# Part products of three image rows: another order for the second image, three products of half width for the third and last

## The chip, the cores and the metric

The kernel runs on one core of a Trainium2 chip. A core has five engines that run beside each other, each with its own queue of instructions in a fixed order: TensorE (PE, matrix products, with weight loads shown as PEld), VectorE (DVE), ScalarE (ACT), GpSimd (POOL) and SyncE (SP, which here only issues transfers). An engine waits at the head of its queue until what it needs is there; everything behind it waits too. The metric is the device time of one execution in microseconds (us), the median of several runs; smaller is better.

## What is computed

The input x has four images of 256 channels and 64 x 64 pixels, in 32-bit floats. Two layers follow each other.

1. Local attention. A 7 x 7 convolution with dilation 2 (128 outputs, then a 1 x 1 convolution to 49) gives 49 logits for each pixel; a softmax over the 49 gives weights; the output at a pixel is the sum of the 49 dilated neighbours of x, each by its weight:

```
k = conv(x, w1, dilation 2, padding 6) + b1        # 4 x 128 x 64 x 64
k = conv(k, w2, 1 x 1) + b2                        # 4 x 49 x 64 x 64
attn = softmax(k, over the 49)
y[b, c, h, w] = sum over (u, v) of x_padded[b, c, h + 2u, w + 2v] * attn[b, (u, v), h, w]
```

2. Whitening. The 256 channels of y are taken in four groups of 64. Each group's covariance over all pixels of all images is formed, its inverse square root is found by five Newton steps, and the group's channels are multiplied by it.

## The kernel before

Both convolutions are merged into one with 49 outputs of 7 x 7 taps over 256 channels. Because the dilation is 2, rows and columns of equal parity form four independent convolutions of 32 x 32 pixels. Each is done by a fast convolution in two dimensions (Toom-Cook): rows and columns are evaluated at seven points 0, 1, -1, 2, -2, 1/2 and infinity (`EVAL`, `INF = 6`), products are taken for each pair of a row point and a column point, and the output is interpolated, first along columns (`col_interp`), then along rows (`row_interp`).

**Row points.** For the row points 1, -1, 2, -2, 1/2 (and 0 for the later images) a row of products is made in three banks (`conv_bank`, matmuls at line 604, two halves of the partitions for the two row parities): DVE makes the column points (`xh`), PE multiplies, ACT copies the result out of PSUM into `pv` (lines 615 and 620), and DVE interpolates it into `zz`. The row points at infinity, and 0 in the first two images, need no evaluation of rows. There the 7-tap convolution along the columns is taken directly from the pixels: `direct` does it with seven products of whole rows (matmuls at line 779). `direct_part` (matmuls at line 862) does it with three products of half width, in two column classes: with even and odd column pairs x0 and x1 and even and odd taps w0 and w1, part 1 is w1 on x0, part 2 is w0 on x1, and part 3 is the sum of both tap classes on the sum of both pixel classes. `direct_sums` makes the sums on DVE, and `direct_ends` puts the three products together (ACT copies part 1, DVE adds part 2 twice and subtracts from part 3). In the kernel before, the second image uses the three products for its row points infinity and 0; the third and fourth use `direct`, called from `direct_inf`.

**Order of the work.** Images overlap. While image b is convolved, image b - 1 goes through softmax (`soft`), through the moves of its weights into a band shape (ACT copies into `zt` at line 1253, stores to `sd` in DRAM issued by POOL at line 1272, loads of `band` and `bandz` issued by SP at lines 1322 and 1334), and through the weighted sum on PE (line 1442, with blocks of pixels that PE has transposed at line 1378), whose results are turned (line 1514) and multiplied into the covariance (line 1533). A list of steps with costs per image (line 1703 and on) places the pieces of image b - 1 between the convolution steps of image b; `steps.insert` puts the direct rows and the softmax at its start. Within that frame a scheduler orders the instructions of each engine by priority. On DVE part of the order is written out: `add`, `sub` and `madd` (lines 345 to 352) go through `in_turn`, which makes each of them stand behind the last one that was issued while `strict` was on. `in_order` turns `strict` on around an image's last interpolations (`col_interp`, then `row_interp(b, 1)`).

**Memory that the change touches.** `spare` is the third part of `pv`; its first 686 elements hold the weights of the row at infinity of the next image (`kept[INF]`, loaded by SP at line 899), and the part behind them is a temporary of `col_interp`. `lgx` holds the weights of the second image's row 0 (`gr0`) while they are needed, and the logits of an image afterwards. `acc` are two banks of PSUM that the weighted sums use later; `conv_psum()` gives the two convolution banks in turn. `tap`, `gbr` and `gb5` lie in a pool (`gpool`) that is released at the end of the front part, and whose memory then holds `zt`, `band` and the softmax terms.

Of the kernel before, what the change touches and what calls it, by code (L numbers as in the profile page):

```python
# [9 lines left out]
F32 = mybir.dt.float32  # L10
# [13 lines left out]
INF = 6  # L24
# [8 lines left out]
def kernel(  # L33
# [310 lines left out]
    def add(o, a, b):  # L344
        return in_turn(TT(o, a, b, ALU.add))  # L345
# [409 lines left out]
    def direct(b, br, s, ps, w, xr=None):  # L755


        a = 3 if br == INF else 0
        order = [(v, cc) for v in sorted(range(KS), key=lambda v: abs(v - R)) for cc in range(NCC)]
        for j, (v, cc) in enumerate(order):  # L760
            d = 2 * (v - R)
            w0, w1_ = max(0, -d), min(W, W - d)
            for h in range(2):
                if xr is not None:
                    parts = [(w0, w1_, xr[:, :, h, cc, w0 + d : w1_ + d])]
                elif b == 0:
                    xs = slots[h].rearrange("p c (q a) w -> p a q c w", a=4)[:, a]
                    parts = [(w0, w1_, xs[:, :, cc, w0 + d : w1_ + d])]
                else:
                    xs = halves(slots[2 * b + h])[:, cc].rearrange("p h (q a) w -> p a h q w", a=4)  # L770
                    parts = []
                    for g in range(2):
                        i0, i1 = max(w0 + d, g * SW), min(w1_ + d, (g + 1) * SW)
                        parts.append(
                            (i0 - d, i1 - d, xs[:, a, g, :, i0 - g * SW : i1 - g * SW])
                        )
                for k, (o0, o1, rhs) in enumerate(parts):
                    pe(
                        nc.tensor.matmul(  # L779
                            ps[h * HB : h * HB + KT, :, o0:o1],  # L780
                            w[v][:, cc],
                            rhs,
                            start=(j == 0 and k == 0),
                            stop=(j == len(order) - 1),
                            skip_group_check=True,
                        )
                    )
        z = zz[:K2, br]
        if s == 0:
            with tc.high_priority():  # L790
                nc.scalar.copy(z[:, :Q8], ps[:K2])
        else:

            def second():
                nc.scalar.copy(z[:, Q8], ps[:K2, Q8 - 1])
                add(z[:, 1:Q8], z[:, 1:Q8], ps[:K2, : Q8 - 1])

            if br == 0 and b == 0:

                seconds.append(second)  # L800
            else:
                second()

    M16, NX = W // 4, Q8 * 2 * NCC * W // 2

    def direct_sums(b, br, w, room):

        a = 3 if br == INF else 0
        xs = []
        for h in range(2):  # L810
            x = slots[2 * b + h].rearrange("p c r w -> p (c r w)").rearrange(
                "p (e a w) -> p a e w", a=4, w=SW
            )
            x = x[:, a].rearrange("p e (m i two) -> p i e m two", i=2, two=2)
            o = room[:, h * NX // 2 : (h + 1) * NX // 2]
            add(o.rearrange("p (e m two) -> p e m two", m=SW // 4, two=2), x[:, 0], x[:, 1])
            xs.append(
                o.rearrange("p (c g q w) -> p c g q w", c=NCC, g=2, q=Q8).rearrange(
                    "p c g q (m two) -> p c g q m two", two=2
                )  # L820
            )
        ws = []
        for s, t in enumerate(w):
            nw = (KS // 2) * NCC * KT
            o = room[:, NX + s * nw : NX + (s + 1) * nw]
# [50 lines left out]
    def direct_view(ps, n, m):  # L876
        return ps.rearrange("p q w -> p (q w)")[:, : n * m * 2].rearrange(
            "p (q m two) -> p q m two", q=n, two=2
        )

    def direct_ends(br, n, p1, p2, p3=None):

        z = zz[:K2, br, :n].rearrange("p q (m i two) -> p i q m two", i=2, two=2)
        if p3 is None:
            nc.scalar.copy(z[:, 0], p1[:K2])
            add(z[:, 1], z[:, 0], p2[:K2, :, 1:])
            add(z[:, 0], z[:, 0], p2[:K2, :, :M16])
        else:
            sub(z[:, 1], p3[:K2], z[:, 1])
# [3 lines left out]
    def conv_psum():  # L893
        ncv[0] += 1
        return cv_buf[(ncv[0] - 1) % 2].rearrange("p (q w) -> p q w", w=W)

    def direct_inf(b):

        nc.sync.dma_start(spare[:, :NTAP], kept[INF])
        t = spare[:, :NTAP].rearrange("p (v a k) -> p v a k", v=KS, a=NCC)  # L900
        direct(b, INF, 0, conv_psum(), [t[:, v] for v in range(KS)])

    start_of = {}

    def direct_start(sr):

        n = Q8 + 1
        w = [[gr0[:, v, :, s] for s in range(2)] for v in range(KS)]
        if sr == 0:
            room = store[4].rearrange("p c r w -> p (c r w)")[:, SH * W :]  # L910
            xs, ws = direct_sums(1, 0, [[t[s] for t in w] for s in range(2)], room)
            start_of["xs"] = xs
            start_of["ws"] = [[t[j] for t in ws] for j in range(KS // 2 + 1)]
# [10 lines left out]
    acc = [ps_y.tile([P, Q8, W], F32, tag="y", name=f"acc{sr}") for sr in range(2)]  # L924
    for a in acc:
        nc.vector.memset(a, 0.0)
# [779 lines left out]
    for b in range(1, B):  # L1706

        steps = []
        for k, (bk, br) in enumerate(rows):
            if bk == b:  # L1710
                for i, cost in enumerate((6, 5, 2)):
                    steps.append((cost, lambda k=k, i=i: conv_step(k, i)))
        if b == 1:
            for sr in range(2):
                steps.insert(sr, (12, lambda sr=sr: direct_start(sr)))
            steps.insert(0, (0, lambda: soft(0, 0)))
            steps.insert(3, (0, lambda: soft(0, 1)))
        else:
            steps.insert(0, (12, lambda b=b: direct_inf(b)))
        j, at, whole = 0, 0, sum(c for c, _ in steps)  # L1720
        for cost, f in steps:
            half_next[0] = (at + cost) * NPC >= (j + 1) * whole and (b, j) in half_gaps
            f()
            while rest_of:
                rest_of.pop()()
            at += cost
            if at * NPC >= (j + 1) * whole:
                gap(b, j)
                j += 1
                while after_gap:  # L1730
                    after_gap.pop()()
# [302 lines left out]
```

## Time and profile before

| what | value |
| --- | --- |
| median of 3 runs | 668.89 us (668.85 to 669.1) |
| profiled execution | 668.98 us, span of its instructions 667.2 us |
| mean granted clock of PE | 0.991 |
| second image's row at infinity: parts 2 and 1 (112 matmuls), part 3 (64) | 6.36 us, 3.49 us |
| second image's row 0: parts 2 and 1 (224 matmuls) | 12.42 us |
| third and fourth image's row at infinity: `direct` (112 matmuls each) | 273.02 to 284.61 and 409.00 to 420.58 us |
| first weighted sum on PE | 186.57 us |

One matrix product of 32-bit floats is two matmul instructions in the trace. A row of the profile gives its start, its length, the engine, the line of the kernel, the operation with what it writes and reads, the shape, the count of merged instructions, and in brackets how long the engine had stood idle and what ended that. Lines 345, 348 and 352 are the helpers `add`, `sub` and `madd`, so these rows are told apart by the tile that they write.

### The profile page before, as it was taken

Reading aid. Unit: us, or ns where it says so; the run is one execution under the profiler, and the core shown is the slowest. Engines: PE = TensorE matmul, PEld = TensorE weight load, DVE = VectorE, ACT = ScalarE, POOL = GpSimd, SP = SyncE. Lnnn points to the kernel's source line nnn. Section 1 sums busy time; section 2 is a strip of 40 time slices with the busy share of each in tenths; the row PEclk is TensorE's granted clock in tenths of the full one; section 3 lists DMA queues with packets and bytes.
Section 4 is the critical chain, followed back from the end, with each engine's and each line's share of the span. In section 5 each row is a group of like instructions: output and inputs, shape, how many; then the busy total and the mean of one; then the engine's idle time right before and its main releaser. Section 6 shows DMA issues by size and latency. Waiting matters only on the chain.

```text
span 667.2 us, 19415 instructions
## 1 busy us (share of the span) xinstructions
PE 638.7 (96%) x7992; PEld 530.1 (79%) x7992; DVE 571.2 (86%) x1258; ACT 331.8 (50%) x861; POOL 115.3 (17%) x173
## 2 busy tenths in 40 slices
PE   6999999999999999999999999999999999999991
PEld 1439673358999998889999998999999999997440
DVE  3699999999899889999999799989999988634781
ACT  1434331013565566467754554473855667535681
POOL 0000551663213002001022020002220203500000
PEclk9999999999999999999999999999999999999996
DMA  8961799995599988324588673026364325739698
GB/s 316 247 177 67 128 232 382 218 195 83 133 205 223 228 257 304 103 57 108 149 278 278 232 246 107 1 69 195 103 197 112 70 65 129 182 96 380 263 412 335
DMA packets 109840, 126.11 MB, mean 189 GB/s; under 512 B 69127, under 2 KB 92216, under 8 KB 107576
## 3 DMA queue, kind: packets, MB, share of 16 engines
q1 hardware_dynamic: 92952, 69.35, 35.5%
q0 software_dynamic: 10752, 37.26, 21.7%
q10 hardware_dynamic: 6048, 18.27, 8.8%
q8 instruction: 63, 1.03, 0.7%
q14 instruction: 25, 0.20, 0.1%
HBM read 78.78 MB, written 52.36 MB: 197 GB/s over the span
## 4 chain that ended last, share of the span: by engine, by line
PE 62%; DVE 17%; issue 7%; POOL 4%; SPq 4%; DMA 3%; ACT 2%; DVEq 0%; ACTq 0%; POOLq 0%
PE cv L604 25%; PE y L1442 13%; PE sig L1533 5%; PE tp L1514 4%; PE tp L1378 4%; SPq L225 4%; POOL ahead L147 2%; POOL slot L147 2%; PE tp L1844 2%; PE cv L862 2%; DVE zz L352 2%; DVE rb L345 2%; PE cv L779 2%; DVE xh L352 2%; DVE pv L352 1%
## 5 line engine op out<-in xcount | busy, mean ns | idle before, releaser
L604 PE MATMUL cv<-xh,wr 128*49 128x128 f32 x4160 | 232.3, 273 | 0.1
L604 PEld LDWEIGHTS cv<-xh,wr 128*49 128x49 f32 x4160 | 226.2, 124 | 2.9 <-issue 1.0
L1272 POOL DMA_DIRECT2D sd<-zt x120 | 63.3, 534 | 292.2 <-ACT zt L1253 222.2
L1442 PE MATMUL y<-band,xb 128*128 128x209 f32 x448 | 93.7, 341 | 0.6 <-ACT xb L1409 0.6
L1442 PEld LDWEIGHTS y<-band,xb 128*128 128x128 f32 x448 | 75.7, 191 | 1.5 <-ACT xb L1409 0.8
L615 ACT COPY pv<-cv 113x486 f32<-113x486 f32 (+2 forms) x60 | 25.9, 431 | 82.4 <-PE cv L604 82.2
L352 DVE SCALAR_TENSOR_TENSOR pv<-pv 113x162 f32<-113x162 f32 x176 | 52.5, 320 | 1.5 <-ACT pv L615 1.0
L1524 ACT COPY yt<-tp 128x512 f32<-128x512 f32 x60 | 35.0, 591 | 24.3 <-PE tp L1514 23.5
L1253 ACT COPY zt<-d 32x112 f32<-32x112 f32 (+2 forms) x132 | 38.6, 293 | 11.0 <-DVE d L1123 5.1
L1514 PE MATMUL tp<-ident,slot 128*128 128x128 f32 x240 | 41.3, 295 | 0.2 <-ACT slot L1464 0.2
L1378 PE MATMUL tp<-ident,slot 128*128 128x128 f32 x256 | 40.5, 282 | 0.0
L1175 ACT ACTIVATE d<-tp,mx 128x49 f32<-128x49 f32 x96 | 27.4, 321 | 24.2 <-DVE mx L1172 17.6
L1533 PE MATMUL sig<-yt 128*64 128x65 f32 x1024 | 38.0, 225 | 0.9 <-ACT yt L1524 0.9
L1514 PEld LDWEIGHTS tp<-ident,slot 128*128 128x128 f32 x240 | 34.9, 205 | 5.0 <-issue 3.7
L1378 PEld LDWEIGHTS tp<-ident,slot 128*128 128x128 f32 x256 | 38.2, 204 | 0.2 <-issue 0.2
L1533 PEld LDWEIGHTS sig<-yt 128*64 128x64 f32 x1024 | 32.9, 137 | 6.7 <-issue 1.9
L1409 ACT COPY xb<-tp 128x512 f32<-128x512 f32 x52 | 30.6, 588 | 13.7 <-PE tp L1378 10.5
L352 DVE SCALAR_TENSOR_TENSOR xh<-ct 128x512 f32<-128x512 f32 x40 | 26.6, 691 | 5.7 <-PE cv L604 5.4
L147 POOL DMA_DIRECT2D slot<-in_x_dram x12 | 20.4, 1701 | 53.4 <-DVE xh L352 38.6
L348 DVE TENSOR_TENSOR pv<-pv 113x162 f32<-113x162 f32 (+1 forms) x77 | 27.5, 364 | 0.3
L352 DVE SCALAR_TENSOR_TENSOR xh<-xh,rb 128x512 f32<-128x512 f32 x40 | 27.4, 684 | 0.1
L345 DVE TENSOR_TENSOR ct<-rb 128x1024 f32<-128x1024 f32 (+1 forms) x26 | 26.5, 1020 | 0.3
(288 smaller groups left out, 1141.9 us busy)
## 6 DMA issues: line engine op xcount, KB each, us to landing
band<-sd SPq DMA_DIRECT2D x64, 242.0 KB, 3.6
sd<-zt POOLq DMA_DIRECT2D x120, 77.0 KB, 4.2
wr<-gd ACTq DMA_DIRECT2D x14, 588.0 KB, 4.8
wr<-gd ACTq DMA_DIRECT2D x14, 490.0 KB, 4.1
slot<-in_x_dram POOLq DMA_DIRECT2D x12, 512.0 KB, 10.5
ahead<-in_x_dram POOLq DMA_DIRECT2D x12, 512.0 KB, 7.8
spill<-slot POOLq DMA_DIRECT2D x3, 2048.0 KB, 9.4
slot<-ahead POOLq DMA_DIRECT2D x3, 2048.0 KB, 10.7
```

What stands on the lines that cost most here:

```text
L147: yield queue.dma_start(o[:, cc, h], src[:, :, pr, h * SW : (h + 1) * SW])
L345: return in_turn(TT(o, a, b, ALU.add))
L352: return in_turn(STT(o, a, f, b, ALU.mult, ALU.add))
L604: nc.tensor.matmul(o, wv[:, sc, sr, cc], xv[bc][:, h * NCC + cc], start=(j == 0), stop=(j == len(terms) - 1), skip_group_check=True,)
L1253: ins = nc.scalar.copy(o, i)
L1272: dma = queue.dma_start(bass.AP(tensor=D.tensor, offset=D.offset + h * HS + g * RS, ap=[[LS, TC], [CR * RS, NCH], [1, KS * WS]],), zt[p0 : ...
L1378: nc.tensor.transpose(t[:, h * C + cc * P : h * C + (cc + 1) * P], tile_of(xt, cc, t8, h, pc), turned_by(n),)
L1409: (nc.vector.tensor_copy if n > 4 * B - 3 else nc.scalar.copy)(xb.rearrange("p a c -> p (a c)"), t[:, : 2 * C])
L1442: nc.tensor.matmul(y_ps[n, half, cc][:, q0 : q0 + nq, c0:c1], xb[:, cc * P : (cc + 1) * P], rhs, start=(k == 0), stop=(k == len(PIECES[hal ...
L1514: nc.tensor.transpose(t[:, h * C + cc * P : h * C + (cc + 1) * P], tile_of(yt, cc, t8, h, pc), turned_by(n),)
L1524: return nc.scalar.copy(yb.rearrange("p h a g c -> p (h a g) c")[:, :, :GW], t[:, : 2 * C].rearrange("p (e c) -> p e c", c=GW),)
L1533: nc.tensor.matmul(sig[g * GW : (g + 1) * GW, cc], yb[:, g, :GW], yb[:, g], start=(count[0] == 0), stop=end, skip_group_check=True,)
```

## The change

It has three parts. First, the second image: the parts 2 and 1 of its row at infinity are taken earlier, straight after the first image's last direct product, and the sums for its part 3 are made after the first image's row interpolation, into `spare` and the last third of `lgx`; part 3 itself moves behind the parts 2 and 1 of row 0, into `direct_start(1)` (`third_inf`). Second, the step of the first softmax, `soft(0, 0)`, moves from before `direct_start(0)` to behind it. Third, `direct_inf` of the third and the last image makes the three products of half width in place of the seven whole ones: parts 1 and 2, then part 3 in the bank of part 1, with the sums in the free part of `pv` and behind the weights in `spare`, and a memset on POOL that restores the zeros there. Besides, the tap sums are made by one addition (`direct_taps`) where there were three or six.

```diff
-    def direct_sums(b, br, w, room):
+    def direct_sums(b, br, w, room, sums):
...
-        ws = []
-        for s, t in enumerate(w):
-            nw = (KS // 2) * NCC * KT
-            o = room[:, NX + s * nw : NX + (s + 1) * nw]
-            o = o.rearrange("p (v a k) -> p v a k", v=KS // 2, a=NCC)
-            for j in range(KS // 2):
-                add(o[:, j], t[2 * j + 1], t[2 * j])
-            ws.append([o[:, j] for j in range(KS // 2)] + [t[KS - 1]])
-        return xs, ws
+        return xs, direct_taps(w, sums)
+
+    def direct_taps(w, sums):
+
+        n = w.shape[2]
+        o = sums[:, : KS // 2 * n].rearrange("p (v n) -> p v n", n=n)
+        pair = w[:, : KS - 1].rearrange("p (v two) n -> p two v n", two=2)
+        add(o, pair[:, 1], pair[:, 0])
+        return [o[:, j] for j in range(KS // 2)] + [w[:, KS - 1]]
...
         nc.sync.dma_start(spare[:, :NTAP], kept[INF])
         t = spare[:, :NTAP].rearrange("p (v a k) -> p v a k", v=KS, a=NCC)
+        if b in (2, 3):
+            free = pv[:, 1 - (len(slot) - NV) % 2]
+            with tc.high_priority():
+                xs, ws = direct_sums(
+                    b, INF, t.rearrange("p v a k -> p v (a k)"),
+                    free.rearrange("p n q b -> p (n q b)"), spare[:, NTAP:],
+                )
+            one = lambda t: [t.rearrange("p (a k) -> p a k", a=NCC)]
+            p2 = direct_view(conv_psum(), Q8, M16 + 1)
+            bank = conv_psum()
+            p1 = direct_view(bank, Q8, M16)
+            w = [[t[:, v]] for v in range(KS)]
+            direct_part(b, INF, 1, p1, w)
+            direct_part(b, INF, 2, p2, w)
+            with tc.high_priority():
+                direct_ends(INF, Q8, p1, p2)
+            p3 = direct_view(bank, Q8, M16)
+            direct_part(b, INF, 3, p3, [one(t) for t in ws], xs)
+            with tc.high_priority():
+                direct_ends(INF, Q8, None, None, p3)
+            nc.gpsimd.memset(
...
+            )
+            return
         direct(b, INF, 0, conv_psum(), [t[:, v] for v in range(KS)])
...
         else:
-            p3 = direct_view(acc[0], n, M16)
+            third_inf()
+            p3 = direct_view(acc[1], n, M16)
             direct_part(1, 0, 3, p3, start_of["ws"], start_of["xs"])
             direct_ends(0, n, None, None, p3)
 
+    def third_inf():
+
+        p3 = direct_view(acc[0], Q8, M16)
+        direct_part(1, INF, 3, p3, start_of["ws_inf"], start_of["xs_inf"])
+        direct_ends(INF, Q8, None, None, p3)
...
     prepare(NR0, 0)
-    w = [tap[:, UPOS[3], v] for v in range(KS)]
-    xs, ws = direct_sums(1, INF, [w], gbr.rearrange("p v a s k -> p (v a s k)"))
     direct0(5, 1)
+    g = tap[:, UPOS[3]].rearrange("p v a k -> p v (a k)")
+    one = lambda t: [t.rearrange("p (a k) -> p a k", a=NCC)]
+    p2 = direct_view(acc[0], Q8, M16 + 1)
+    direct_part(1, INF, 2, p2, [one(g[:, v]) for v in range(KS)])
+    p1 = direct_view(acc[1], Q8, M16)
+    direct_part(1, INF, 1, p1, [one(g[:, v]) for v in range(KS)])
     row_interp(0, 1)
-
-    w = [[t] for t in w]
-    p2 = direct_view(acc[0], Q8, M16 + 1)
-    direct_part(1, INF, 2, p2, w)
-    p1 = direct_view(acc[1], Q8, M16)
-    direct_part(1, INF, 1, p1, w)
-    p3 = direct_view(conv_psum(), Q8, M16)
-    direct_part(1, INF, 3, p3, [[t] for t in ws[0]], xs)
+    direct_ends(INF, Q8, p1, p2)
+    room = lgx[:, 2 * KS * NCC * KT :]
+    start_of["xs_inf"], ws = direct_sums(1, INF, g, spare, room)
+    start_of["ws_inf"] = [one(t) for t in ws]
     prepare(NR0, 1)
     prepare(NR0, 2)
     strict[0] = False
-    direct_ends(INF, Q8, p1, p2)
-    direct_ends(INF, Q8, None, None, p3)
+    last_tap = room[:, KS // 2 * NCC * KT :][:, : NCC * KT]
+    nc.scalar.copy(last_tap, g[:, KS - 1])
+    start_of["ws_inf"][-1] = one(last_tap)
     gpool.release()
...
         if b == 1:
             for sr in range(2):
                 steps.insert(sr, (12, lambda sr=sr: direct_start(sr)))
-            steps.insert(0, (0, lambda: soft(0, 0)))
+            steps.insert(1, (0, lambda: soft(0, 0)))
             steps.insert(3, (0, lambda: soft(0, 1)))
```

More of the change, by code (lines that the diff above doesn't have):

```diff
@@ L900, in direct_inf @@
         t = spare[:, :NTAP].rearrange("p (v a k) -> p v a k", v=KS, a=NCC)
+        if b in (2, 3):
[19 more added lines that the diff above has]
+            nc.gpsimd.memset(
+                free[:, ORDER.index(INF)].rearrange("p q b -> p (q b)").rearrange(
+                    "p (q c) -> p q c", q=Q9
+                )[:, :, 2 * Q8 :],
+                0.0,
+            )
+            return
         direct(b, INF, 0, conv_psum(), [t[:, v] for v in range(KS)])
+    acc = [ps_y.tile([P, Q8, W], F32, tag="y", name=f"acc{sr}") for sr in range(2)]
+    for a in acc:
+        nc.vector.memset(a, 0.0)
     start_of = {}
@@ L907, in direct_start @@
         n = Q8 + 1
-        w = [[gr0[:, v, :, s] for s in range(2)] for v in range(KS)]
         if sr == 0:
+            by_share = lambda t: [
+                t.rearrange("p (a s k) -> p a s k", a=NCC, s=2)[:, :, k] for k in range(2)
+            ]
+            g = lgx[:, : KS * 2 * NCC * KT].rearrange("p (v n) -> p v n", v=KS)
             room = store[4].rearrange("p c r w -> p (c r w)")[:, SH * W :]
-            xs, ws = direct_sums(1, 0, [[t[s] for t in w] for s in range(2)], room)
+            xs, ws = direct_sums(1, 0, g, room, room[:, NX:])
             start_of["xs"] = xs
-            start_of["ws"] = [[t[j] for t in ws] for j in range(KS // 2 + 1)]
+            start_of["ws"] = [by_share(t) for t in ws]
+            w = [by_share(g[:, v]) for v in range(KS)]
             p2 = direct_view(conv_psum(), n, M16 + 1)
@@ L919, in direct_start @@
         else:
-            p3 = direct_view(acc[0], n, M16)
+            third_inf()
+            p3 = direct_view(acc[1], n, M16)
             direct_part(1, 0, 3, p3, start_of["ws"], start_of["xs"])
             direct_ends(0, n, None, None, p3)
-    acc = [ps_y.tile([P, Q8, W], F32, tag="y", name=f"acc{sr}") for sr in range(2)]
-    for a in acc:
-        nc.vector.memset(a, 0.0)
+    def third_inf():
+        p3 = direct_view(acc[0], Q8, M16)
+        direct_part(1, INF, 3, p3, start_of["ws_inf"], start_of["xs_inf"])
+        direct_ends(INF, Q8, None, None, p3)
     rows = [(0, br) for br in (1, 2, 3)]
```

## The prediction

> **What bounds the kernel now.** I read the page's busy shares first, then busy time by stage, then the order of time of PE and DVE around the three changed places, and last what ended each engine's waits. Busy shares of the 667.2 us span, then three stages (after the range and its length: busy us of PE, PEld, DVE, ACT and POOL with counts, then the granted clock):
>
> ```profile
> PE 638.7 (96%) x7992; PEld 530.1 (79%) x7992; DVE 571.2 (86%) x1258; ACT 331.8 (50%) x861; POOL 115.3 (17%) x173
> ...
> 176.80:273.00 96.20, 94.75 (x1409) 91.71 (x1409) 86.94 (x202) 59.09 (x158) 13.77 (x26) 1.00 0.93 235
> 273.00:285.00 12.00, 12.00 (x123) 9.12 (x118) 12.00 (x35) 2.54 (x6) 0.00 (x0) 1.00 0.21 73
> 285.00:409.00 124.00, 123.18 (x1808) 119.42 (x1808) 117.25 (x242) 77.45 (x222) 17.03 (x32) 1.00 0.61 194
> ```
>
> From 142 us to about 545 us PE hardly waits, so PE work taken away there is time, and so is every new wait put into its queue. But DVE is nearly as full: in the stage 273 to 285, where the third image's row at infinity runs, it has no gap at all. So a sum that the change gives to DVE counts as soon as PE needs it at once. PE in order of time (start, length, what; in brackets its wait):
>
> ```profile
> 142.50 6.36 PE L862 MATMUL acc<-slot,tap 128*49 128x128 f32 x112
> 149.80 2.72 PE L862 MATMUL cv<-gbr 128*49 128x128 f32 x48 [0.94 <-DVE gbr L345]
> 154.94 1.21 PE L1135 MATMUL tp<-ident,slot 113*128 113x113 f32 x8 [1.65 <-ACT slot L746]
> ...
> 186.57 0.98 PE L1442 MATMUL y<-band,xb 128*128 128x209 f32 x4
> ...
> 273.02 11.66 PE L779 MATMUL cv<-slot,pv 128*49 128x256 f32 x112
> ```
>
> DVE at the ends of the images' row interpolation (the lgx rows), and the two places where it last waited for PE before:
>
> ```profile
> 247.52 0.64 DVE L352 SCALAR_TENSOR_TENSOR wr<-ct 128x196 f32<-128x196 f32 x2 [2.71 <-PE cv L604]
> 284.51 0.69 DVE L352 SCALAR_TENSOR_TENSOR lgx<-zz 113x512 f32<-113x512 f32 x1
> ...
> 382.44 0.69 DVE L352 SCALAR_TENSOR_TENSOR xh<-ct 128x512 f32<-128x512 f32 x1 [4.33 <-PE cv L604]
> 418.42 0.69 DVE L352 SCALAR_TENSOR_TENSOR lgx<-zz 113x512 f32<-113x512 f32 x1
> ```
>
> These waits tie DVE's clock to PE's: if PE is late, DVE is late too, and the lag between them at the lgx rows stays as it is.
>
> **Part 1: the third image's row at infinity.** Removed: 112 matmuls of about 256 columns, 273.02 to 284.61, 11.6 us. Added: 176 of half width. The second image's same row gives the price: its parts 2 and 1 (112 matmuls) took 6.36 us, its part 3 (64) 3.49 us, both together 9.9 us. So PE's own work falls by 1.7 us.
>
> But part 3 needs two sums of pixels and one of weights from DVE. They pass through the helper that holds DVE's written order, and in the built order they stand right after the last step of the row interpolation, the lgx row at 284.51. That step gives way after 0.61 us (distance to the next row), at 285.1. Then two sums of 512 (1.21 us, the distance that the two gbr sums took at 148.02), one addition of 256 (0.33, from 160.59 to 160.92) and the weight sum of 294 elements (0.45, between the rows of 162 with 0.32 and 324 with 0.49): 287.1. PE has finished parts 1 and 2 at 273.0 + 6.4 = 279.4 and has nothing else to do: the third product stands next in its queue, and all later matmuls behind it. It waits 7.7 us, runs 3.5 us, and is done at 290.6 instead of 284.6: 6.0 us late. A wait of 0.57 us for ACT at 288.29 goes, since ACT has time meanwhile. **Step: +5.5 us.**
>
> DVE pays 2.6 us more than before here (the sums above, 0.33 for the second addition, 0.4 for the subtraction of part 3), yet PE is 5.5 us late, and at 382.44 DVE had 4.3 us to spare. So this costs nothing more. ACT copies 256 elements instead of 512: less work. POOL gets a memset of 18 elements after part 3; it issued nothing from 255 to 312 us, nor from 391 to 450 behind the last image's. SP's load of the next image's weights moves from 284.7 to about 290.7 and the store behind it on SP moves along; the weights are wanted at 409, so this is hidden.
>
> **Part 2: the last image, same steps.** Parts 1 and 2: 409.0 + 6.4 = 415.4. The lgx row at 418.42 gives way at 419.0; sums until 421.0; part 3 until 424.5, instead of 420.6. The wait is 5.6 us. **Step: +4.0 us.** DVE is tied to PE at 382 to 386, so the lag is that of before.
>
> **Part 3: the second image.** PE's queue now runs: infinity parts 2 and 1 (to 148.9), first row's parts 2 and 1 (12.4, to 161.3), eight transposes for the first softmax (1.2), infinity part 3 (3.5), first row's part 3 (6.7), four and eight transposes (1.7): convolution starts at 174.6 and not at 176.83. The waits of 0.94 and 1.65 us go; 2.2 us are gained, and the 88 products before the first weighted sum (9.74 us) end at 184.4.
>
> The first softmax, however, now stands behind 12.4 us of products on PE, and DVE's maximum of it behind steps that used to come later. DVE from 148.02: interpolation tail 4.3, two additions 0.7, infinity sums 1.6, column steps of ct and xh 4.5, first row's sums 1.2 + 0.7 (one addition of 588 where six of 98 were), three rb and ct steps 4.5: the maximum at 165.4 (before: 155.91). Maximum 1.0, sixteen exponentials 4.6, scaling 1.6, shuffles 3.1: ready at 176.0 (before 166.73), 9.3 us late. Behind it hangs this chain (ACT copies, POOL stores, SP loads of the band):
>
> ```profile
> 166.84 3.33 ACT L1253 COPY zt<-d 128x56 f32<-128x56 f32 x11 [5.11 <-DVE d L1123]
> ...
> 169.62 4.21 POOL L1272 DMA_DIRECT2D sd<-zt  x8 [12.66 <-issue]
> ...
> 176.94 0.91 SPq L1322 DMA_DIRECT2D band<-sd  x2
> ```
>
> All 9.3 us later: band issued at 186.2, landed 3.7 us after (median of the band loads in 165 to 192), at 189.9. Before, it landed at about 180.6, and PE first used it at 186.57: 6 us of cover. Now PE is there at 184.4 and waits 5.5 us. **Step: 189.9 - 186.57 = +3.3 us**; ends: -2.2 us if the band is in time, +5 us if the band takes 5.4 us to land, between that median and the longest of all, 8.1. The weight load for the third image moves on SP from 126.5 to about 166, is wanted at 273, and costs nothing.
>
> **Part 4: PE's clock after a wait.** No wait of PE in the middle of this trace reaches 2 us, and the granted clock is 1.00 throughout. What a longer one does is seen only behind PE's last matmul, which ends at 652.85:
>
> ```profile
> 654.00:655.00 1.00, 0.00 (x0) 0.00 (x0) 0.00 (x0) 0.00 (x0) 0.00 (x0) 1.00 0.96 401
> 655.00:656.00 1.00, 0.00 (x0) 0.00 (x0) 0.00 (x0) 0.00 (x0) 0.00 (x0) 0.80 1.01 418
> 656.00:657.00 1.00, 0.00 (x0) 0.00 (x0) 0.00 (x0) 0.00 (x0) 0.00 (x0) 0.50 1.10 459
> ```
>
> The clock falls to 0.50 at 655.6, 2.75 us after the last work. The three new waits (5.5, 7.7, 5.6 us) are all longer. How long half speed lasts once work returns, no row shows. Bounds: nothing, if it returns at once; 2.75 us of loss each, if it takes twice as long to rise as to fall. I take the middle, as long as the fall, an estimate: 2.75 us at half speed, 1.4 us lost each, **+4.1 us** for three.
>
> [...]
>
> **Sum.** The profiled execution took 668.98 us (span 667.2 and 1.8 around it), 0.09 above the median of 668.89. 5.5 + 4.0 + 3.3 + 4.1 = 16.9; 668.89 + 16.9 = **685.8 us**. PE's lateness is carried to the end, since DVE's last chain starts at 512.32 from a copy that waited for PE (0.64 us of slack).
>
> **Rivals.** (a) *The sums are in time and it gets faster.* Only if DVE reached the lgx row 7.7 us sooner against PE; then each image gains 1.7, the front 2.2, if the band is also in time: 668.9 - 5.6 = 663.3. Against it: DVE has no gap from 247.5 to 285. 3 in 100. (b) *The clock does not fall or is back at once:* 681.7. For it: the fall needs 2.75 us and waits may be shorter than worked out. 25 in 100. (c) *The band is in time*, because softmax starts sooner than my walk along DVE's queue says; then -2.2 in place of +3.3 and one clock loss less: 678.9. Against it: 9.3 us of delay meet 6 us of cover. 17 in 100. (d) *Clock losses at the upper bound:* 8.3 in place of 4.1, or a band landing late: 690. 15 in 100. The likeliest holds 40.
>
> **Range.** From (c) to a little over (d): 677 to 691; the likeliest alone is 683 to 688. Within 0.2% (1.3 us, about what a measurement of this kernel can tell from no change) needs the gain of (a) to meet one of the losses: 1 in 100. Faster 3, slower 96.
>
> **What would show it.** Right: PE waits of 5 to 8 us for DVE pv ahead of the third products near 280 and 420, and one for a band DMA near 185; granted clock under 1 just behind them; part rows of 9.9 us in place of 11.6. Wrong: third products without a gap, or PE gaps that DVE's order explains but which later waits give back.

## The result, and the profile after

The changed kernel takes 690.6 us (median of five runs, 689.4 to 691.0) against 669.0 us, a ratio of 1.0318 with a 95% interval of 1.0303 to 1.0333. That is 21.6 us slower where 16.9 were forecast: the direction and the three places are as predicted, and the size lies at the upper end of the range (677 to 691), outside the likeliest case (683 to 688). The profiled execution has a span of 689.0 us against 667.2: 21.8 us to explain.

The busy shares of the changed kernel's page:

```profile
PE 642.1 (93%) x8120; PEld 538.2 (78%) x8120; DVE 576.6 (84%) x1263; ACT 333.1 (48%) x862; POOL 115.4 (17%) x175
```

PE has 3.4 us *more* busy time than before although the three products of half width are less work. That alone says that some products ran slowly. The stages, with the same columns as before (range and its length; busy us of PE, PEld, DVE, ACT, POOL with counts; granted clock; DMA share; GB/s):

```profile
183.60:279.30 95.70, 87.39 (x1234) 84.37 (x1234) 83.51 (x195) 55.51 (x136) 13.76 (x26) 0.96 0.98 231
279.30:299.30 20.00, 11.86 (x185) 11.45 (x179) 19.82 (x54) 4.75 (x10) 0.00 (x0) 0.74 0.18 69
299.30:423.60 124.30, 123.76 (x1809) 119.81 (x1809) 112.33 (x228) 76.10 (x218) 17.12 (x33) 1.00 0.60 189
423.60:442.00 18.40, 12.57 (x185) 12.16 (x181) 16.17 (x34) 2.31 (x5) 0.00 (x0) 0.81 0.07 18
```

The third image's row at infinity now fills a stage of 20 us in which PE works 11.9 us and DVE 19.8; the last image's fills 18.4 us. In both the clock is well under 1 (0.74 and 0.81), and between them PE is full as it was. PE in order of time around the three places (start, length, what; in brackets its wait):

```profile
173.80 9.81 PE L604 MATMUL cv<-xh,wr 128*49 128x128 f32 x176
190.47 1.73 PE L1481 MATMUL y<-band,xb 128*128 128x209 f32 x4 [6.85 <-DVE xh L352]
...
197.80 2.39 PE L604 MATMUL cv<-xh,wr 128*49 128x128 f32 x40
...
279.32 6.35 PE L862 MATMUL cv<-slot,pv 128*49 128x128 f32 x112
293.81 5.56 PE L862 MATMUL cv<-pv 128*49 128x128 f32 x64 [8.14 <-DVE pv L345]
299.29 0.75 PE L1553 MATMUL tp<-ident,slot 128*128 128x128 f32 x4
...
423.65 6.35 PE L862 MATMUL cv<-slot,pv 128*49 128x128 f32 x112
435.83 6.21 PE L862 MATMUL cv<-pv 128*49 128x128 f32 x64 [5.83 <-DVE pv L345]
```

Three waits of 6.9, 8.1 and 5.8 us stand where the prediction put them, and the rows right behind each are long: four weighted sums take 1.73 us instead of 0.98, the third products 5.56 and 6.21 us, where the second image's same 64 take 3.49. The list puts the first wait down to DVE's step xh, but that step ends at 190.46, when PE's weight load for the sums had already begun (190.44). The band's first load, issued at 185.43, landed after 4.9 us, at 190.33, and so it is the band that came last. Its chain of ACT's copies, POOL's stores and SP's loads:

```profile
176.36 3.33 ACT L1292 COPY zt<-d 128x56 f32<-128x56 f32 x11 [5.12 <-DVE d L1162]
...
179.13 4.21 POOL L1311 DMA_DIRECT2D sd<-zt  x8 [20.77 <-issue]
...
185.43 1.85 SPq L1361 DMA_DIRECT2D band<-sd  x2
```

They are 9.5, 9.5 and 8.5 us later than before (166.84, 169.62, 176.94), where 9.3 was worked out. For the two images, DVE has no gap between the last row of logits (lgx) and the sums:

```profile
291.06 0.68 DVE L352 SCALAR_TENSOR_TENSOR lgx<-zz 113x512 f32<-113x512 f32 x1
291.67 1.28 DVE L345 TENSOR_TENSOR pv<-slot 128x512 f32<-128x512 f32 x2
...
293.20 0.46 DVE L345 TENSOR_TENSOR pv<-pv 128x294 f32<-128x294 f32 x1
...
433.08 0.69 DVE L352 SCALAR_TENSOR_TENSOR lgx<-zz 113x512 f32<-113x512 f32 x1
433.69 1.28 DVE L345 TENSOR_TENSOR pv<-slot 128x512 f32<-128x512 f32 x2
```

Now the clock, in stretches of one microsecond (the number behind POOL's count is the granted clock):

```profile
188.00:189.00 1.00, 0.00 (x0) 0.00 (x0) 1.00 (x4) 0.00 (x0) 0.00 (x0) 0.93 1.06 377
...
195.00:196.00 1.00, 1.00 (x6) 0.99 (x5) 0.00 (x0) 0.65 (x2) 0.00 (x0) 0.66 1.62 149
...
287.00:288.00 1.00, 0.00 (x0) 0.00 (x0) 1.00 (x3) 0.00 (x0) 0.00 (x0) 0.92 0.30 113
...
298.00:299.00 1.00, 1.00 (x24) 1.00 (x22) 1.00 (x5) 0.00 (x0) 0.00 (x0) 0.96 0.00 0
...
434.00:435.00 1.00, 0.00 (x0) 0.00 (x0) 1.00 (x3) 0.53 (x1) 0.00 (x0) 0.81 0.00 0
...
441.00:442.00 1.00, 1.00 (x17) 0.82 (x13) 0.00 (x0) 0.00 (x0) 0.00 (x0) 0.78 0.00 0
```

These are the six microseconds in which the clock changes; between each pair it is 0.50. A mean of 0.93 between 1.00 and 0.50 means that it fell after 0.86 of that microsecond, so at 188.86. The others give 195.68 (back), 287.84 (fall), 298.08 (back), 434.62 (fall), 441.44 (back). The distances are 6.82, 92.16, 10.24, 136.54 and 6.82 us, which are 2, 27, 3, 40 and 2 times 3.413 us. So all six changes lie on one grid: in this run the clock changed at the ends of stretches of 3.41 us (called windows below), wherever PE's waits began and ended. In the run with the softmax moved and the sums on POOL (673.4 us, below) means of 0.78 (287 to 288) and 0.52 (290 to 291) put a fall at 287.56 and the return at 290.96, 3.40 us apart, one such window.

The L604 row behind the first weighted sums is the mark by which the front part is compared. Before the change:

```profile
191.53 8.72 PE L604 MATMUL cv<-xh,wr 128*49 128x128 f32 x156
```

Where the 21.8 us are, by the rows above and those of before:

| place | wait and order, forecast | measured | half clock, forecast | measured |
|---|---|---|---|---|
| second image | +3.3 | +3.9 (190.47 against 186.57) | +1.4 | +2.4 (to the next L604 row: 6.3 in all) |
| third image | +5.5 | +6.3 | +1.4 | +2.1 (5.56 against 3.49) |
| last image | +4.0 | +4.0 | +1.4 | +2.7 (6.21 against 3.49) |
| last band | none | +0.4 (a new wait of 0.44) | | |

The third image's step is 299.29 - 279.32 = 20.0 us against 284.61 - 273.02 = 11.6; less 2.1 of half clock, 6.3. The last one's is 18.3 against 11.6; less 2.7, 4.0.

### The profile page after: what moved, and what is told of

It reads as the page before. It is cut to its first block, busy times and chain, and to the rows that moved or that the text cites. A ratio compares the mean times of both kernels' runs of the same rounds, so it can differ in the third digit from the quotient of the medians.

```text
span 689.0 us, 19682 instructions
## 1 busy us (share of the span) xinstructions
PE 642.1 (93%) x8120; PEld 538.2 (78%) x8120; DVE 576.6 (84%) x1263; ACT 333.1 (48%) x862; POOL 115.4 (17%) x175
## 4 chain that ended last, share of the span: by engine, by line
PE 66%; DVE 23%; issue 3%; ACT 3%; DMA 3%; POOL 0%; ACTq 0%; SPq 0%; DVEq 0%; POOLq 0%
PE cv L604 26%; PE y L1481 11%; PE acc L779 7%; PE sig L1572 4%; DVE zz L352 3%; PE tp L1553 3%; PE tp L1417 3%; DVE pv L352 2%; PE cv L251 2%; DVE zz L348 2%; DVE ct L352 2%; PE tp L1883 2%; DVE xh L352 2%; DVE zz L345 2%; PE cv L862 2%
## 5 line engine op out<-in xcount | busy, mean ns | idle before, releaser
L604 PE MATMUL cv<-xh,wr 128*49 128x128 f32 x4160 | 232.3, 273 | 0.1
L604 PEld LDWEIGHTS cv<-xh,wr 128*49 128x49 f32 x4160 | 226.1, 124 | 3.0 <-issue 1.0
L1481 PE MATMUL y<-band,xb 128*128 128x209 f32 x448 | 95.5, 346 | 7.1 <-DVE xh L352 6.9
L1481 PEld LDWEIGHTS y<-band,xb 128*128 128x128 f32 x448 | 77.2, 194 | 8.2 <-issue 7.4
L1553 PE MATMUL tp<-ident,slot 128*128 128x128 f32 x240 | 41.3, 295 | 0.2 <-ACT slot L1503 0.2
L1553 PEld LDWEIGHTS tp<-ident,slot 128*128 128x128 f32 x240 | 34.9, 205 | 4.6 <-issue 3.1
L1448 ACT COPY xb<-tp 128x512 f32<-128x512 f32 x52 | 30.4, 586 | 16.6 <-PE tp L1417 13.5
```

The costliest lines, as they stand in the source:

```text
L604: nc.tensor.matmul(o, wv[:, sc, sr, cc], xv[bc][:, h * NCC + cc], start=(j == 0), stop=(j == len(terms) - 1), skip_group_check=True,)
L1481: nc.tensor.matmul(y_ps[n, half, cc][:, q0 : q0 + nq, c0:c1], xb[:, cc * P : (cc + 1) * P], rhs, start=(k == 0), stop=(k == len(PIECES[hal ...
L1553: nc.tensor.transpose(t[:, h * C + cc * P : h * C + (cc + 1) * P], tile_of(yt, cc, t8, h, pc), turned_by(n),)
```

## Experiments

All times are medians beside the kernel before on the same chip (669.0 to 669.2 us).

### Each place by itself

The second image's new order alone:

```
-        if b in (2, 3):
+        if b in ():
             free = pv[:, 1 - (len(slot) - NV) % 2]
```

> The second image's new order alone; the third and the last image's row at infinity run as before the change. Theory (the three places cost independently of each other): the trace of after shows the front 6.3 us late (first L604 row behind the first weighted sum at 197.80 against 191.53), so 669.0 + 6.3 = 675.3 us, with a wait of about 7 us ahead of the first weighted sum and a stretch at half clock behind it. Rival (the front's lateness is given back later, and the two images cost the whole 21.6): 669 to 671 us.

Measured: 675.4 us (ratio 1.0076 to 1.0106). The next L604 row stands at 197.44 us against 191.53 before, 5.9 late, and PE's last matmul ends 6.2 us late. The other half is the kernel before with only the two images' rows changed (the new branch of direct_inf, with the new direct_sums beside the old one):

```
+        if b in (2, 3):
+            free = pv[:, 1 - (len(slot) - NV) % 2]
...
+                xs, ws = direct_sums2(b, INF, ...)
...
+            return
         direct(b, INF, 0, conv_psum(), [t[:, v] for v in range(KS)])
```

> The kernel before with the third and the last image's row at infinity in three products, its second image unchanged. Theory (the three places cost independently of each other, and half clock adds 2 to 3 us at each wait according to where the clock's fixed windows fall): PE waits 8 and 5.8 us for DVE's sums as in after, 669.0 + 15.2 = 684.2 us (after less the run with the front alone), give or take 1. Rival (half clock costs 1.4 us at each wait, as the prediction had it): 669.0 + 5.5 + 4.0 + 2.8 = 681.3 us.

Measured: 684.3 us (1.020 to 1.0239), waits of 7.89 and 5.82 us for DVE's sums and third products of 5.32 and 5.88 us. 6.4 and 15.2 us add up to 21.6, which is the whole change: the front and the two images cost independently of each other. The third products take 1.8 and 2.4 us longer than 3.49, what the next run shows for them at a clock of 1.00 (here its mean is 0.68 from 287 to 293, where the third image's run), so half clock cost more than 1.4 us a wait.

### Is it the clock that makes the rows behind the waits long?

Part 2 of the two images is repeated while PE has nothing to do. Each repeat begins its sum anew, so that only idle time is filled:

```
             direct_part(b, INF, 1, p1, w)
+            direct_part(b, INF, 2, p2, w, few=4 if b == 2 else 2)
+            direct_part(b, INF, 2, p2, w)
             direct_part(b, INF, 2, p2, w)
```

> After, with part 2 of the two images' products repeated on PE while it waits for DVE's sums (two further times for the third image, one and a half for the last; the repeats compute the same values again, so only PE's idle time is filled). Theory (the third products run slowly because the clock falls in the wait): they take 3.5 us each and not 5.6 and 6.2, so 690.6 - 2.1 - 2.7 = 685.8 us; the sums arrive when they did. Rival (they run slowly since DVE writes beside them or because of the operands): 690.6 us, with rows as long as before.

Measured: 689.55 us (1.0288 to 1.0322), only 1.1 less than after, and the two intervals overlap. PE in order of time:

```profile
294.12 3.49 PE L863 MATMUL cv<-pv 128*49 128x128 f32 x64 [0.76 <-DVE pv L345]
...
339.86 1.76 PE L1484 MATMUL y<-band,xb 128*128 128x209 f32 x4 [2.41 <-DMA band<-sd]
...
438.03 3.49 PE L863 MATMUL cv<-pv 128*49 128x128 f32 x64 [0.19 <-DVE pv L345]
```

The rows say yes: with PE kept busy (its clock is 1.00 from 279 to 298, around the first of them), the same 64 products take 3.49 us both times, right behind the same sums, and DVE writes beside them as before. The images' steps shrink by 2.4 and 3.0 us. The total does not follow. Behind the third image stands a new wait, for the band of the second softmax: from the L604 row of 176 to that of 208 (324.86 to 346.51) it is 21.7 us, where it was 16.6 before and 17.4 in after. The shuffles of DVE that this band hangs on begin at 319.65, as in after (319.68), while PE is there 1.8 us sooner. So DVE, which the change made late, is what PE meets next. 4.3 us go there between the two images, waits and slow rows behind them together (the four weighted sums at 339.86 take 1.76 us instead of 0.98). So the half clock of the third image is real, but taking it away frees little: it covered DVE.

### The place of the first softmax

Ahead of the first row's products again, as before the change:

```
-            steps.insert(1, (0, lambda: soft(0, 0)))
+            steps.insert(0, (0, lambda: soft(0, 0)))
```

> After, with the first softmax put ahead of the first row's products again, as it stands before the change; the rest of the new order stays. Theory (the band is late because the softmax stands behind 12.4 us of products): the band lands before PE has finished its 88 products at about 184.2, the front becomes 2.2 us faster than before instead of 6.3 us slower: 690.6 - 8.5 = 682.1 us, half clock at the two images alone. Rival (the sums of the first row or of the row at infinity, now behind the softmax on DVE, come too late for the third products): a new wait of 2 to 5 us for DVE near 165, 684 to 688 us.

Measured: 688.1 us (1.026 to 1.0291), 6 us above the theory. The band is in time, but PE in order of time has a wait that neither theory named:

```profile
153.07 1.30 PE L1174 MATMUL tp<-ident,slot 113*128 113x113 f32 x8 [4.38 <-ACT slot L746]
154.30 14.09 PE L862 MATMUL cv<-slot,lgx 128*49 128x128 f32 x224
```

The transposes need the row of logits that ACT writes only then, and everything stands behind them in PE's queue. The 224 products behind take 14.09 us where they take 12.59 in after, 1.5 us more; that a lower clock made them slow is my estimate, from the length of the row. 4.4 and 1.5 us are the 6 that are missing. Before the change the 48 products from gbr stood there and left 1.65 us of that wait. The next step puts the softmax behind part 2, which covers it:

```
             direct_part(1, 0, 2, p2, w)
+            soft(0, 0)
             p1 = direct_view(conv_psum(), n, M16)
...
-            steps.insert(1, (0, lambda: soft(0, 0)))
```

> After, with the first softmax between the first row's part 2 and part 1. In the run with the softmax ahead of both, PE waited 4.4 us for ACT's row of logits, until 153.07; part 2 reaches to 155.4, so that wait is covered. Theory (only the place of the softmax makes the band late): PE runs as in after until its 88 products end at 183.6; the softmax starts 6.9 us sooner than in after, the band is there at about 183.6 instead of 190.5, no half clock behind it: 690.6 - 6.9 - 2.4 = 681.4 us, 682.5 if the band is a microsecond late. Rival (DVE, not the band, is what PE meets next: what the front gains is waited for again at the sums of the third image): the wait near 285 grows from 8.1 to 11 us or more, 684 to 688 us.

Measured: 682.2 us (1.0172 to 1.0204), as the theory had it. The waits at the images' sums are 7.93 and 5.81 us, so they did not grow: DVE waits 2.7 us for PE at 245.7 here, as it did at 247.5 in the kernel before, and so gets sooner with PE. The front is now 1.8 us faster than before (the L604 row at 189.71 against 191.53), with 1.23 us of wait left. The last of this series puts the softmax behind three of part 2's four shifts, with images three and four as before the change:

```
         for i, (wt, d) in enumerate(order):
+            if mid and i == 3:
+                mid()
...
-            direct_part(1, 0, 2, p2, w)
+            direct_part(1, 0, 2, p2, w, mid=lambda: soft(0, 0))
```

> The second image's new order alone, images three and four as before the change, and the first softmax behind three of the four shifts of the first row's part 2 (part 2 begins at 148.6 and takes 7.2 us, so at about 154.0; the logits are there at 153.07). Theory (what the new order saves on PE, 2.2 us, is there once the band is in time): with the softmax behind part 2 the band was 1.2 us late and the front no faster than before; 1.4 us and more of DVE steps sooner it is in time, and the front is 1.2 us faster: 667.8 us. Rival (DVE's second softmax or the row steps that now come later hold PE next): 668.5 to 670 us.

Measured: 666.3 us, ratio 0.9953 with an interval of 0.994 to 0.9967: faster than both kernels, by 2.8 us against the one before. PE in order of time:

```profile
148.79 5.55 PE L864 MATMUL cv<-slot,lgx 128*49 128x128 f32 x96
154.27 1.21 PE L1176 MATMUL tp<-ident,slot 113*128 113x113 f32 x8
...
183.79 0.98 PE L1483 MATMUL y<-band,xb 128*128 128x209 f32 x4
...
188.75 5.45 PE L604 MATMUL cv<-xh,wr 128*49 128x128 f32 x96
```

No row has a wait: the logits are there when the transposes come, and the band (issued at 179.10) when the weighted sums come. The L604 row is 2.8 us sooner than before, exactly what the total gains. The theory expected 1.2 us, the rival less. The theory took the front of the run before for no faster than the kernel before; it was 1.8 us faster already, and the 1.2 us of wait come on top. So the second image's new order does save PE's time; the softmax's place in it is what turned 2.8 us of gain into 6.4 of loss.

### The sums in time

The two images' sums go to POOL. The weights' sums go to other buffers, since DVE's column steps use the old one:

```
-            add(o..., x[:, 0], x[:, 1])
...
+            if b > 1:
+                nc.gpsimd.tensor_tensor(o4, x[:, 0], x[:, 1], ALU.add)
+            else:
+                add(o4, x[:, 0], x[:, 1])
...
+        if b > 1:
+            o = [zeros[:, :n], zeros[:, n : 2 * n], room[:, NX : NX + n]]
+            for j in range(KS // 2):
+                nc.gpsimd.tensor_tensor(o[j], w[:, 2 * j + 1], w[:, 2 * j], ALU.add)
...
```

> After, with the two images' sums of pixels and weights computed on POOL, which issues nothing between its band stores near 262 and the row's end, instead of in DVE's written order. Theory (the sums come late only because they stand behind the row interpolation on DVE): they are ready before PE has done parts 1 and 2 at 279, no wait, no half clock: both rows take 9.9 us instead of 11.6, so 690.6 - (8.4 + 1.7) - (6.7 + 1.7) = 672 us. Rival (the sums wait for the buffer that they are written to, which the last convolution row gives free, or POOL is too slow for them): PE still waits 3 us or more at each, 680 to 690 us.

Measured: 683.0 us (1.018 to 1.0216). POOL and then DVE in order of time:

```profile
287.40 2.93 POOL L819 TENSOR_TENSOR pv<-slot 128x512 f32<-128x512 f32 x2 [1.08 <-DVE zz L352]
...
287.84 1.59 DVE L352 SCALAR_TENSOR_TENSOR zz<-zz 113x576 f32<-113x576 f32 x1
```

The rival's reason holds: POOL waits until DVE's last column step gives the buffer free, at 287.4. PE then waits 3.1 and 0.9 us for the third image's sums, 1.1 and 1.1 for the last one's. So the sums were late for two reasons, DVE's written order and their target buffer. Now the other of the two buffers, which the row before the last has left:

```
-            free = pv[:, 1 - (len(slot) - NV) % 2]
+            free = pv[:, (len(slot) - NV) % 2]
```

> The sums on POOL as before, but written to the other of the two buffers, which the row before the last has given free, instead of the one that DVE's last column step held until 287.4. Theory (the sums were late for that buffer alone): POOL has them near 266 and 405, PE does not wait for them, both rows take 9.9 us: 672 us. Rival (DVE, which is late by its share of the new steps, is met next at the band of the second softmax behind the third image, as PE's wait of 3.1 us for it near 336 to 340 in the run with repeated products): 674 to 677 us.

Measured: 680.6 us (1.013 to 1.0186), worse than both expected. The wait for the sums is gone, and the three parts run without a gap from 279.09 to 288.68 and from 418.81 to 428.66, 2.0 and 1.7 us less than before. But the time comes back elsewhere: 2.5 us of wait for ACT's copy xb at 294.27, a few rows behind the third image's, 1.9 us for the second softmax's band at 331.1 with slow rows behind it (four weighted sums in 1.76 us instead of 0.98; 20.3 us from one L604 row to the next instead of 16.6), 1.3 us for ACT at 462.3. With the softmax between part 2 and part 1 as well (both edits shown above, nothing else):

> Both: the softmax between part 2 and part 1, and the sums on POOL in the other buffer. Theory (the three waits are all that the change costs, and what is left is its saving of 2.2 us in the front and 1.7 us in each image): 668.9 - 2.2 - 3.4 = 663.3 us. Rival (DVE has no room for a faster PE: the saving turns into waits for bands, lgx rows and column steps): 667 to 671 us.

Measured: 673.4 us (1.0041 to 1.0077), still slower than before. The DVE, ACT and PE rows of the moment where the third image's saving is lost:

```profile
285.10 0.68 DVE L352 SCALAR_TENSOR_TENSOR lgx<-zz 113x512 f32<-113x512 f32 x1
...
285.82 0.72 ACT L746 ACTIVATE lgx<-lgx,bias 113x512 f32<-113x512 f32 x1 [2.23 <-DVE lgx L352]
286.44 0.57 ACT L1459 COPY xb<-tp 128x512 f32<-128x512 f32 x1
...
287.06 1.32 PE L1492 MATMUL y<-band,xb 128*128 128x209 f32 x4 [2.28 <-ACT xb L1459]
```

PE has finished the row at infinity 2.9 us sooner than in the kernel before (281.68 against 284.61) and waits for a copy that stands on ACT behind the row of logits, and ACT waits there for DVE. In the kernel before, DVE began that step at nearly the same time (284.51), and PE already waited 0.57 us for the same copy:

```profile
287.66 0.58 ACT L1409 COPY xb<-tp 128x512 f32<-128x512 f32 x1
...
288.29 0.98 PE L1442 MATMUL y<-band,xb 128*128 128x209 f32 x4 [0.57 <-ACT xb L1409]
```

From the start of the row at infinity to these weighted sums PE took 15.27 us there (273.02 to 288.29) and takes 14.97 here (272.09 to 287.06). So of the 2.0 us that PE saves in the row, 0.3 are left. Where PE waits already, work taken from it ahead of the wait makes the wait longer, unless the copy comes sooner too.

Two more runs took the front of 666.3 us with these images, and then moved ACT's copy xb ahead of the row of logits (a dependence that orders the two on ACT):

```
-            else:
-                end()
+            elif b in (1, 2) and a == 1:
+                after_xb.append(end)
+            else:
+                end()
...
+        while after_xb and t8 == 1:
+            tc.add_manual_dep(after_xb.pop()().ins, copied.ins.name, ..., reason="after_xb")
```

> The softmax behind three of four shifts of part 2 (the front that ran at 666.3 us with images three and four as before), and the two images' rows in three products with their sums on POOL in the other buffer. Theory (DVE has no room for a faster PE in the two images: PE waits about 2.3 us for ACT's copy xb, which stands on ACT behind the row of logits that DVE finishes near 285, and the savings of 1.7 us are lost): as in the run with the softmax one shift later, where the two images cost 3.3 - (-0.9) = 4.2 us, so 666.3 + 4.2 = 670.5 us. Rival (the images save their 1.7 us each once the front is in time): 663 us.

> The same, and ACT copies xb before the last part of the row of logits, so that PE no longer stands behind DVE there. Theory (that copy's place on ACT is what takes the third image's saving): the wait of 2.3 us near 285 and the half clock behind it go, 666 to 668 us. Rival (DVE itself is late, and PE meets it next at the band of the second softmax near 315 or at the logits' transposes near 293): the wait moves there, 669 to 671 us.

Measured: 670.4 us (1.0005 to 1.0025) and 671.1 us (1.0008 to 1.0031). The first has the theory's number. In the second the wait moves, as its rival said, though near 288 it moved to a copy and not to the transposes; PE in order of time:

```profile
287.98 0.69 PE L1503 MATMUL y<-bandz,xbz 128*128 128x96 f32 x4 [1.99 <-ACT xbz L1454]
...
322.29 0.97 PE L1503 MATMUL y<-band,xb 128*128 128x209 f32 x4 [1.22 <-DMA band<-sd]
```

The first run's number, though, came by the theory's reason only in part. Its wait at the copy is there (2.20 us, and the four weighted sums behind it take 0.97 us, so they are not slow), yet of the 4.1 us between 666.3 and 670.4 about 1.5 are lost long before, in the front. POOL and then PE, first of the run at 666.3, then of the one at 670.4:

```profile
172.06 4.21 POOL L1313 DMA_DIRECT2D sd<-zt  x8 [13.44 <-issue]
...
173.01 2.86 POOL L830 TENSOR_TENSOR zeros<-pv 128x98 f32<-128x98 f32 x2
175.81 3.14 POOL L1323 DMA_DIRECT2D sd<-zt  x6
...
185.29 0.95 PE L1493 MATMUL y<-band,xb 128*128 128x209 f32 x4 [1.57 <-DMA band<-sd]
```

The third image's weight sums (`zeros`, 2.86 us) stand in POOL's queue between the first softmax's stores. The band is issued 1.8 us later (180.94 against 179.10), and the next L604 row stands at 190.22 instead of 188.75; the run at 671.1 has the same. The run at 673.4 has it too, 0.9 us against the same front without the sums on POOL (190.60 against 189.71). No run has these sums behind the stores, so whether the 1.5 us come back is open.

The rest is small gains that are given back (by the L604 rows of the two runs). From the row at infinity to the next L604 row the third image is 0.4 us faster than in the run at 666.3 and the last one 1.0. Against that stand, among smaller ones, 0.9 us at the second softmax's band and a new wait of 1.4 us for ACT's copy at 451.70. So in the versions tried the two images' new row gains nothing, with no wait for the sums either: 666.3 us without it, 670.4 with it, of which 1.5 belong to the place of POOL's weight sums.

## Why the prediction was right, and where it was not

**Part 1, the third image.** Right in its mechanism and nearly in its size: a wait of 8.1 us against 7.7, parts 2 and 1 in 6.35 against 6.4. Wrong in a small thing: the 0.57 us of wait for ACT were counted as a gain. From the L1553 row to the next L604 row PE does gain 0.84 us (7.58 against 8.42), but it loses 0.82 on the way to the L604 row of 208 (17.37 against 16.55), at the second softmax's band. The sentence that DVE's 2.6 us "costs nothing more" fails there too, and the run with the repeated products shows what lies under PE's lateness once that is gone: 4.3 us, half clock included. The price of PE's own work was a little off as well: 1.7 us of saving in a row, where 2.0 and 1.7 were measured without a wait.

**Part 2, the last image.** Right: 4.0 us, a wait of 5.8 against 5.6.

**Part 3, the second image.** Right: the softmax's place delays the band. The step was 3.9 us and not 3.3, since the band landed 4.9 us behind its issue instead of 3.7; it was issued at 185.43 and not 186.2. The remedy tried last confirms the other side of the step: with the band in time the new order gains 2.8 us, where 2.2 were worked out. The walk along PE's queue added up the lengths of rows, which overlap by 0.1 to 0.2 us each: it came to 174.6 where after has 173.80.

Some sums of the prediction are off by 0.1 to 0.3 us. PE's walk adds up to 174.4 and not 174.6, the softmax's to 175.7 and not 176.0, DVE's extra steps to 2.7 and not 2.6, and the third image's step to 5.4 and not 5.5. None of them decides anything.

**Part 4, the clock.** This is the term that was mis-sized: 4.1 us forecast, 7.2 measured (2.4, 2.1, 2.7). It makes 3.1 of the 4.9 us that are missing. The step that failed is "I take the middle, as long as the fall". One fall behind the last matmul, after 2.75 us, was taken for a delay that starts when PE stops, with a rise equally long. No such delay shows in after. The clock fell 5.2, 2.2 and 4.6 us after PE's last work, each time at the end of a window of the grid, and stayed low until a window had passed that was full of work (192.27 to 195.68, 294.67 to 298.08 and 438.03 to 441.44, PE busy for 3.41 us in each): 5.2, 4.3 and 5.6 us after the work came back, about half of each lost. In these three waits the work came back in the middle of a window, and the rest of that window (1.8, 0.9 and 2.2 us) ran at 0.50 on top of the whole next one.

**The rivals.** (d), upper losses of clock or a late band, was the nearest: both came in part. (a), sums in time, named 663.3 us; the run that has them in time and the band 2.0 us late gave 673.4, the one with the best front 670.4. Its price took PE's saving at full value and did not ask what PE would meet: ACT's copy behind DVE's row of logits, on which the kernel before already waited 0.57 us. (c), the band in time, named 678.9; with the softmax behind part 2 it measured 682.2. The front gave nearly its part (1.8 us of gain for 2.2), and the images were dearer, by their clock above all: 15.2 us alone where 12.3 follow from the prediction's terms.

## What to carry to other kernels

When PE work is cut in a stage, look for waits that PE already has behind it, however small: where one stands, PE is early already, and a saving ahead of it is worth only what its releaser gains too, here 0.3 us of 2.0. When work is put ahead of a step on an in-order queue, follow that step's whole chain to its last user, and look for the place where its input has just arrived and no earlier: here the softmax's place turned a gain of 2.8 us into a loss of 6.4, and placing it too early cost 4.4 us of wait for the logits and 1.5 of slower products behind it. When work is moved to an idle engine, see what it then stands ahead of: here POOL's sums for a later image made the first band late. An idle time of PE of 4 to 8 us cost 1.5 to 2.7 us of slower products behind it here, one of about 2 us nothing or up to 1.7; covering it with spare products shows what it costs (here 3.49 us for the 64 products instead of 5.56 and 6.21).

## What the runs showed of the hardware

The six changes of PE's clock in after lie on a grid of windows of 3.41 us, and the window ahead of a fall was not always wholly idle. That of 284.43 to 287.84 held 1.2 us of work, and the clock fell at its end; that of 427.79 to 431.21 held 2.2 us, and it stayed at 1.00; that of 188.86 to 192.27 held 1.8 us, and it stayed at 0.50. So I estimate that the place of a wait on this grid can decide whether it costs clock. Two runs have such a wait for ACT's xb, 2.48 us (sums on POOL, other buffer) and 2.28 us (with the softmax moved). In the first (range and length, PE's busy us, clock, DMA share, GB/s) the clock holds:

```profile
292.00:293.00 1.00, 0.00 (x0) 1.00 0.00 0
293.00:294.00 1.00, 0.00 (x0) 1.00 0.00 0
294.00:295.00 1.00, 0.73 (x4) 1.00 0.00 0
```

and in the second, with the shorter wait (284.78 to 287.06, whole in the 3.41 us ahead of the fall at 287.56), it falls 0.5 us after the work returns and stays low for 3.40 us, which costs 1.7 us at 0.50:

```profile
286.00:287.00 1.00, 0.00 (x0) 1.00 0.00 0
287.00:288.00 1.00, 0.94 (x4) 0.78 0.00 0
288.00:289.00 1.00, 1.00 (x6) 0.50 0.00 0
```

Where the first one's wait lies on the grid no row shows. The difference may be why kernels with such waits scatter more: the second one's ten runs lie between 671.0 and 676.7 us, the five of the kernel without them (666.3) between 666.0 and 666.4. But the kernel before, which has no such wait either, lies between 668.8 and 671.1 beside them. This was not tested by itself.

DVE's steps were longer while POOL added, in two runs: a step of 113x576 that takes 0.75 us took 1.59 beside POOL's two additions at 287.40, and the next, 0.35 otherwise, took 1.19. With the other buffer and the softmax moved, steps of 113x576 beside the same additions (POOL at 259.30) took 1.52 and 1.41. The two additions took POOL 2.93 us, DVE 1.28. So at 287.40 DVE lost 1.7 us beside them, more than the 1.28 that it was spared.
